# Attention and a depthwise convolution on one core: column differences of the last tile on GpSimd, rows moved by transfers, a later factor pass

## The chip, the cores and the metric

The kernel runs on one core of a Trainium2 chip. The metric is the device time of one execution in microseconds; lower is better. Several executions are timed and the median is given. One further execution is recorded by the hardware profiler; its page and trace are what is read here.

## The reference

The input `x` has 16 images of 384 channels, 32 by 32 points, in float32. Two layers follow each other.

```python
def _gn(v, G=32, eps=1e-5):          # 32 groups of 12 channels
    g = v.reshape(B_, G, C_ // G, H_, W_)
    m = jnp.mean(g, axis=(2, 3, 4), keepdims=True)
    s = jnp.var(g, axis=(2, 3, 4), keepdims=True)
    return ((g - m) / jnp.sqrt(s + eps)).reshape(v.shape)

x = x + attention(_gn(x))            # 8 heads of 48 channels over 1024 points
w_sym = (w + rot90(w) + rot90(w, 2) + rot90(w, 3)) * 0.25
x = x + depthwise_conv7x7(_gn(x), w_sym)   # one 7 x 7 filter per channel, padding 3
```

The filter is the mean of its four rotations. So it has the same value at (dy, dx) and (-dy, -dx), and each tap can be taken as a part that is even in dx and one that is odd in dx: sums and differences of columns.

## The kernel before

**Tiles.** A tile is 128 channels by 1024 points of one image; an image has three. Attention runs image by image on TensorE with the exponentials on ScalarE. The convolution of an image runs beside the attention of the next ones. VectorE convolves all tiles but three. The three of `PE_TILES` go to TensorE: tile 2 of image 14 (called the first below), then tiles 2 and 1 of image 15. Tile 0 of image 15 is `LAST`, the last tile of VectorE.

**VectorE's way to convolve a tile** (`fold_ops`). The tile lies in `padded`, rows of 32 points with a pitch of 35. `side(j, n, op)` (line 865) makes the sum or the difference of the columns at +j and -j, one `TENSOR_TENSOR` of 128x1024. `into` (line 868) adds a side times a weight to a row buffer, `rows_e` for the even part and `rows_o` for the odd one; `shifted` (lines 882 and 884) adds a row buffer, moved by dy rows, to the output tile. Line 884 is the plain addition; line 882 is taken once `scale` has been filled and multiplies by a factor at the same time.

**The last image is special.** Its normalization factors are known only late. So its tiles are convolved without them, and the factors are put in at the end. `whole` (line 889) is the factor pass of `LAST`: it multiplies the output tile by the factor and adds `rest`, a buffer that holds the tile itself plus a border term. What `shifted` adds after `whole` must carry the factor, by line 882. For `LAST`, ScalarE makes the first term of each odd row buffer (`begin`, line 962), with the sides that VectorE has made just before.

**The factors.** ScalarE sums each channel of image 15 (`moments`); TensorE averages over groups twice (`average`, line 400): first the means, and then, once VectorE has made `d` (lines 411 to 413), the variances. VectorE makes line 417, GpSimd the power (line 418), VectorE lines 421 and 1714. Then ScalarE writes the border terms (line 1727), and GpSimd's queue adds them to `rest` and to the two TensorE tiles (line 1728, accumulating transfers).

**TensorE's way to convolve a tile.** The image's rows are loaded several times at different offsets into the `sh` buffers (`conv_load`, lines 1092 and 1094, eight transfers each), and matmuls with banded matrices follow (`conv_on_pe`, line 1115). The result lies in PSUM with even and odd rows of a channel on different partitions. ScalarE copies it to SBUF (`conv_take`, line 1130), and `conv_perm` brings the rows to their channel by four matmuls with a permutation (line 1141). ScalarE copies that to an SBUF tile (line 1156 with the factor, line 1160 without it), GpSimd's queue adds it to the tile of `x` (line 1161), and SP's queue stores the sum (line 1175). The very last tile, (15, 1), is added by VectorE from PSUM instead (`conv_add`, line 1171), and ScalarE's queue stores it.

**What sets the order.** Every engine runs its instructions in the order in which the program issues them, and waits on semaphores for others. The program is written by a planner with two clocks, one for TensorE and one for VectorE: `after(wait, cost, f)` puts a small piece of work at a due time, `catch_up(to)` issues VectorE's next operations up to a time, with the costs that stand beside them in the list `ops`. The end of the program (`fast_end`) is written by hand: it issues the moments, the copy `rest` (line 1681), the pieces of TensorE's convolution and the two averages; `first` holds the permutations of the first tile until the factors are known. Transfers are issued by SP, ScalarE and GpSimd, each in its own order; a transfer that waits holds back all behind it on its queue.

Of the kernel before, what the change touches and what calls it, by code (L numbers as in the profile page):

```python
# [10 lines left out]
F32 = mybir.dt.float32  # L11
I32 = mybir.dt.int32
AF = mybir.ActivationFunctionType
# [32 lines left out]
def kernel(  # L46
# [96 lines left out]
    def run(general):  # L143
        tag = "g" if general else "f"
        with ExitStack() as stack:
# [710 lines left out]
            def fold_ops(b, k, i):  # L856
# [16 lines left out]
                scale = []  # L873

# [47 lines left out]
                slot = {2: 0, 3: 1, 1: 2}  # L922
                for n, (dy, (j, l)) in enumerate(((1, (2, 3)), (2, (3, 1)), (3, (1, 2)))):
                    sums.append(
                        (ts, lambda dy=dy, j=j, n=n: first(rows_o[n % 2], sides[slot[j]], o(dy, j)))
                    )
                    sums.append(
                        (full, lambda dy=dy, l=l, n=n: into(rows_o[n % 2], sides[slot[l]], o(dy, l)))
                    )
                    out_rows(lambda n=n: rows_o[n % 2], dy, ALU.subtract)  # L930
# [28 lines left out]
                if (b, k) == LAST:  # L959

                    def begin(n, dy, j):
                        nc.scalar.activation(rows_o[n], sides[slot[j]], AF.Identity, scale=o(dy, j))  # L962

                    def side_begin(j, n, dy):
                        side(j, n, ALU.subtract)
                        begin(n, dy, j)

                    def minus_begin():
                        shifted(rows_o[0], -1, ALU.subtract)
                        begin(0, 3, 1)  # L970

                    ops = [op for op in ops if op[1] not in [f for _, f in (*sums[12:], *outs[10:])]]
                    ops += [
                        (full, lambda: side_begin(2, 0, 1), None),
                        (full, lambda: side_begin(3, 1, 2), None),
                        (full, lambda: (sums[14][1](), other_borders()), None),
                        (*sums[16], None),
                        (*sums[18], None),
                        (*outs[10], None),
                        (full, minus_begin, None),  # L980
                        (full, whole, None),
                        (*outs[12], None),
                        (*outs[13], None),
                        (*sums[20], None),
                        *((*f, None) for f in outs[14:]),
                    ]
                return ops

# [143 lines left out]
            def conv_perm(b, k, a):  # L1132

                nonlocal clock
                if a == 0:
                    return
                pss[b, k] = psum(f"ps_rows_{b}_{k}")
                for half in range(2):
                    part = slice(64 * half, 64 * half + 64)
                    for row in range(2):  # L1140
# [8 lines left out]
                if (b, k) == PE_TILES[-1]:  # L1149
                    after(5.0, 1.5, lambda: conv_add(b, k))  # L1150
                    return
                t = tpool.tile([P, N], F32, tag="t", name=f"conv_{b}_{k}")
                if b == B - 1:
                    while "borders" not in late:
                        catch_up(now() + 0.5)
                    nc.scalar.activation(
                        by_rows(t), grids(pss[b, k]), AF.Identity, scale=ends["st"].sc[:, k, 0:1]
                    )
                else:
                    nc.scalar.copy(by_rows(t), grids(pss[b, k]))  # L1160
# [503 lines left out]
            def fast_end(b):  # L1664
# [16 lines left out]
                nc.scalar.copy(grid(ends["x"]), padded_view(n))  # L1681
                after(4.0, 0.3, check_end)
# [179 lines left out]
```

## Time and profile before

| | |
|---|---|
| median of 3 runs | 2838.41 us (2837.36 to 2839.85) |
| the profiled execution | 2837.61 us |
| its span, first to last instruction | 2835.8 us |
| TensorE busy | 2823.5 us (100% of the span) |
| VectorE busy | 2080.8 us (73%) |
| ScalarE busy | 1665.1 us (59%) |
| GpSimd busy | 271.5 us (10%) |
| granted TensorE clock | 0.999 |

In the profile PE is TensorE, DVE is VectorE, ACT is ScalarE, POOL is GpSimd and SP is the sync engine, which issues transfers. A row of a timeline gives the start and the duration in us from the start of the span, then engine, line, operation, the tile that is written and those that are read, their shapes, and the number of instructions that are merged in the row; in brackets stands the idle time before it and what ended it. The busy shares say nothing of the end of the program. There the stretches are:

| stretch, us | TensorE busy | VectorE busy | ScalarE busy | GpSimd busy | mean DMA share |
|---|---|---|---|---|---|
| 2783 to 2799 | 16.00 | 15.93 | 14.17 | 0.00 | 0.50 |
| 2799 to 2810 | 11.00 | 10.89 | 1.60 | 2.58 | 0.41 |
| 2810 to 2828 | 16.50 | 16.82 | 10.20 | 3.65 | 0.90 |
| 2828 to 2836 | 0.00 | 0.20 | 0.00 | 0.00 | 0.47 |

### The profile page before, as it was taken

Reading aid. Unit: us, or ns where it says so; the run is one execution under the profiler, and the core shown is the slowest. Engines: PE = TensorE matmul, PEld = TensorE weight load, DVE = VectorE, ACT = ScalarE, POOL = GpSimd, SP = SyncE. Lnnn points to the kernel's source line nnn. Section 1 sums busy time; section 2 is a strip of 40 time slices with the busy share of each in tenths; the row PEclk is TensorE's granted clock in tenths of the full one; section 3 lists DMA queues with packets and bytes.
Section 4 is the critical chain, followed back from the end, with each engine's and each line's share of the span. In section 5 each row is a group of like instructions: output and inputs, shape, how many; then the busy total and the mean of one; then the engine's idle time right before and its main releaser. Section 6 shows DMA issues by size and latency. Waiting matters only on the chain. (4 is left out here: it accounts for less than half of the span.)

```text
span 2835.8 us, 46155 instructions
## 1 busy us (share of the span) xinstructions
PE 2823.5 (100%) x19356; PEld 1122.2 (40%) x19356; DVE 2080.8 (73%) x2264; ACT 1665.1 (59%) x1954; POOL 271.5 (10%) x450
## 2 busy tenths in 40 slices
PE   9999999999999999999999999999999999999998
PEld 5344343433434334343443434334343343434433
DVE  5502968959598595976959689595985959869788
ACT  3637647376574756647466474765747566474653
POOL 4201011310100001010010100101000010100111
PEclk9999999999999999999999999999999999999999
DMA  6512031211212112121120302112121121211224
GB/s 238 188 37 50 27 81 26 54 50 45 64 32 44 50 44 64 34 64 43 37 65 27 82 24 51 50 44 65 32 44 50 44 64 33 63 45 37 72 72 136
DMA packets 75994, 168.21 MB, mean 59 GB/s; under 512 B 32416, under 2 KB 34400, under 8 KB 74240
## 3 DMA queue, kind: packets, MB, share of 16 engines
q0 software_dynamic: 33856, 111.00, 15.1%
q1 hardware_dynamic: 40912, 52.32, 6.8%
q8 instruction: 154, 2.52, 0.4%
q10 hardware_dynamic: 1008, 1.84, 0.2%
q14 instruction: 64, 0.52, 0.1%
HBM read 112.37 MB, written 27.43 MB: 49 GB/s over the span
## 5 line engine op out<-in xcount | busy, mean ns | idle before, releaser
L646 ACT ACTIVATE e<-ps_s 128x1024 f32<-128x1024 f32 x1024 | 1021.7, 1030 | 448.8 <-PE ps_s L638 443.2
L638 PE MATMUL ps_s<-qk 48*64 48x512 f32 x8192 | 1041.1, 589 | 0.0
L658 PE MATMUL acc<-e,v 64*64 64x512 f32 x8192 | 1040.1, 588 | 0.0
L865 DVE TENSOR_TENSOR side<-padded 128x1024 f32<-128x1024 f32 x270 | 328.6, 1218 | 338.2 <-ACT padded L836 338.2
L868 DVE SCALAR_TENSOR_TENSOR rows_e<-side,even,rows_e 128x1024 f32<-128x1024 f32 x405 | 509.3, 1273 | 85.6 <-ACT rows_e L847 84.0
L638 PEld LDWEIGHTS ps_s<-qk 48*64 48x64 f32 x8192 | 311.0, 132 | 574.3 <-issue 526.5
L658 PEld LDWEIGHTS acc<-e,v 64*64 64x64 f32 x8192 | 312.8, 132 | 569.6 <-issue 569.6
L567 PE MATMUL ps_qk<-x,wqk 128*128 128x512 f32 x1152 | 501.3, 594 | 1.4 <-DVE x L483 1.4
L567 PEld LDWEIGHTS ps_qk<-x,wqk 128*128 128x128 f32 x1152 | 217.6, 190 | 278.5 <-issue 271.3
L884 DVE TENSOR_TENSOR x<-x,rows_e 128x992 f32<-128x992 f32 (+2 forms) x270 | 310.6, 1150 | 0.0
L884 DVE TENSOR_TENSOR x<-x,rows_o 128x992 f32<-128x992 f32 (+2 forms) x266 | 305.1, 1147 | 3.0
L574 ACT COPY qk<-ps_qk 128x1024 f32<-128x1024 f32 x96 | 97.2, 1012 | 318.9 <-PE ps_qk L567 318.9
L593 PE MATMUL ps_v<-wv,x 128*128 128x384 f32 x768 | 252.6, 486 | 0.0
L719 PE MATMUL ps_proj<-o,wp 128*128 128x512 f32 x540 | 234.2, 592 | 0.0
L613 ACT COPY v<-ps_v 64x384 f32<-64x384 f32 x256 | 121.6, 475 | 122.4 <-PE ps_v L593 119.8
L593 PEld LDWEIGHTS ps_v<-wv,x 128*128 128x128 f32 x768 | 145.9, 190 | 108.2 <-issue 14.3
L868 DVE SCALAR_TENSOR_TENSOR rows_o<-side,odd,rows_o 128x1024 f32<-128x1024 f32 x135 | 172.7, 1280 | 2.0 <-ACT rows_o L962 0.5
L994 POOL DMA_DIRECT2D out<-x x44 | 24.9, 565 | 1545.1 <-DVE x L884 1544.4
L868 DVE SCALAR_TENSOR_TENSOR x<-side,even,x 128x1024 f32<-128x1024 f32 x135 | 172.4, 1277 | 0.0
L719 PEld LDWEIGHTS ps_proj<-o,wp 128*128 128x128 f32 x540 | 102.6, 190 | 126.2 <-issue 117.7
L727 ACT ACTIVATE x<-ps_proj,bp 128x1024 f32<-128x1024 f32 x45 | 50.1, 1114 | 167.5 <-PE ps_proj L719 167.5
L847 ACT ACTIVATE rows_e<-padded,even 128x1024 f32<-128x1024 f32 x135 | 146.8, 1167 | 0.0
(177 smaller groups left out, 1045.7 us busy)
## 6 DMA issues: line engine op xcount, KB each, us to landing
x<-in_x POOLq DMA_DIRECT2D x90, 512.0 KB, 5.4
inv<-inv SPq DMA_DIRECT2D x126, 256.0 KB
out<-x POOLq DMA_DIRECT2D x44, 512.0 KB, 3.0
xs<-in_x POOLq DMA_DIRECT2D x42, 512.0 KB, 6.4
qk<-qk POOLq DMA_DIRECT2D x96, 128.0 KB, 4.1
o<-o SPq DMA_DIRECT2D x180, 32.0 KB
sh<-v SPq DMA_DIRECT2D x32, 128.0 KB
sum<-o SPq DMA_DIRECT2D x128, 4.0 KB
```

The costliest lines, as they stand in the source:

```text
L567: nc.tensor.matmul(ps[:, h, :], lhsT=wqk[:, k, s, t, :], rhs=xns[b][:, k, h * HALF : (h + 1) * HALF], start=(k == 0), stop=(k == NK - 1),)
L574: nc.scalar.copy(halves(qks[u][:, s, :]), ps)
L593: nc.tensor.matmul(ps[:, j, 0:C], lhsT=xns[b][:, k, t * P : (t + 1) * P], rhs=wv[:, k, :], start=(k == 0), stop=(k == NK - 1),)
L613: nc.scalar.copy(dst[:, :, 0 : HEADS // 2 * (D + 1)].rearrange("p k (h d) -> p k h d", d=D + 1)[:, :, :, 0:D], src.rearrange("p k (h d) -> ...
L638: nc.tensor.matmul(ps[64 * c : 64 * c + 64, a, :], lhsT=qk[r, 1, 64 * kb : 64 * kb + 64], rhs=qk[r, 0, h * HALF : (h + 1) * HALF], start=True,
L646: nc.scalar.activation(es[n], ps, AF.Exp, scale=SCALE)
L658: nc.tensor.matmul(accs[a][64 * j : 64 * j + 64, :], lhsT=v[rows, kb, c : c + 64], rhs=e[rows, j, :], start=(kb == 0), stop=(kb == 2 * NT ...
L719: nc.tensor.matmul(ps[:, h, :], lhsT=wp[:, t, o * P : (o + 1) * P], rhs=os_[b, t // 2][:, t % 2, h * HALF : (h + 1) * HALF], start=(t == 0 ...
L847: nc.scalar.activation(grid(rows_e[dy - 1]), padded_view(i), AF.Identity, scale=even[:, k, dy, 0:1],)
L865: vec.tensor_tensor(grid(sides[n]), padded_view(i, j), padded_view(i, -j), op)
L868: vec.scalar_tensor_tensor(dst, src, w, dst, ALU.mult, ALU.add)
L884: vec.tensor_tensor(dst, dst, src, op)
```

## The change

It has three parts, all in the work on the last image.

First, the three column differences of `LAST` are made by GpSimd into buffers of their own (`ends["minus_sides"]`, in two buffers of the pool that held attention's outputs), issued in `fast_end` right after the copy `rest`. The two scaled copies that begin the odd row buffers follow at once on ScalarE (`odd_begin`, which takes the place of `begin`).

Second, the permutation matmuls of TensorE's first tile, (14, 2), are replaced by 16 transfers on SP's queue (`conv_rows_by_dma`), SBUF to SBUF, 16 partitions of 512 elements each, into `planes`. ScalarE's copy, GpSimd's accumulation and SP's store of that tile are issued after those of tile (15, 2). The loops of the remaining permutations are swapped: row outside, half inside.

Third, `whole` moves behind the two additions with dy = 2, which are therefore plain ones (line 884) and no longer carry the factor. So four additions of the odd part precede it.

```diff
+                slot = {2: 0, 3: 1, 1: 2}
+
+                def minus(j):
+                    return ends["minus_sides"][j] if (b, k) == LAST else sides[slot[j]]
...
-                    def side_begin(j, n, dy):
-                        side(j, n, ALU.subtract)
-                        begin(n, dy, j)
-
                     def minus_begin():
                         shifted(rows_o[0], -1, ALU.subtract)
-                        begin(0, 3, 1)
+                        odd_begin(0, 3, 1)
...
                     ops += [
-                        (full, lambda: side_begin(2, 0, 1), None),
-                        (full, lambda: side_begin(3, 1, 2), None),
-                        (full, lambda: (sums[14][1](), other_borders()), None),
-                        (*sums[16], None),
+                        (full, lambda: (sums[16][1](), other_borders()), None),
                         (*sums[18], None),
                         (*outs[10], None),
                         (full, minus_begin, None),
-                        (full, whole, None),
                         (*outs[12], None),
                         (*outs[13], None),
+                        (full, whole, None),
                         (*sums[20], None),
...
+            def odd_begin(n, dy, j):
+
+                nc.scalar.activation(
+                    rows_o[n],
+                    ends["minus_sides"][j],
+                    AF.Identity,
+                    scale=odd[:, LAST[1], dy, j : j + 1],
+                )
...
+                if (b, k) == PE_TILES[0]:
+                    conv_rows_by_dma(b, k)
+                    return
                 pss[b, k] = psum(f"ps_rows_{b}_{k}")
-                for half in range(2):
-                    part = slice(64 * half, 64 * half + 64)
-                    for row in range(2):
+                for row in range(2):
+                    for half in range(2):
+                        part = slice(64 * half, 64 * half + 64)
...
+                while "borders" not in late:
+                    catch_up(now() + 0.5)
+                conv_out(b, k, pss[b, k])
+                conv_out(*PE_TILES[0], ends["planes"])
+
+            def conv_rows_by_dma(b, k):
+
+                rows = epool.tile([P, 2, HALF], F32, tag="e", name=f"planes_{b}_{k}")
+                for half in range(2):
+                    for i in range(NG // 2):
+                        for row in range(2):
+                            first = 2 * CG * i + CG * (1 - row)
+                            nc.sync.dma_start(
+                                rows[64 * half + i : 64 * half + 64 : NG // 2, row, :],
+                                shs[b, k][first : first + CG, half, :],
+                            )
+                ends["planes"] = rows
+
+            def conv_out(b, k, rows):
...
                 ends["x"] = flat(epool.tile([P, 2, HALF], F32, tag="e", name="rest"))
                 nc.scalar.copy(grid(ends["x"]), padded_view(n))
+                free = [oqpool.tile([P, 2, N], F32, tag="oq", name=f"minus_{n}") for n in range(2)]
+                ends["minus_sides"] = minus = {}
+                for i, j in enumerate((2, 3, 1)):
+                    minus[j] = free[i // 2][:, i % 2, :]
+                    nc.gpsimd.tensor_tensor(
+                        grid(minus[j]), padded_view(n, j), padded_view(n, -j), ALU.subtract
+                    )
+                odd_begin(0, 1, 2)
+                odd_begin(1, 2, 3)
                 after(4.0, 0.3, check_end)
```

`conv_out` holds the lines that ended `conv_perm` before: ScalarE's copy, GpSimd's accumulation and SP's store of a tile.

More of the change, by code (lines that the diff above doesn't have):

```diff
@@ L921, in fold_ops @@
                     sums.append((full, lambda j=j, n=n: side(j, n, ALU.subtract)))
-                slot = {2: 0, 3: 1, 1: 2}
                 for n, (dy, (j, l)) in enumerate(((1, (2, 3)), (2, (3, 1)), (3, (1, 2)))):
                     sums.append(
-                        (ts, lambda dy=dy, j=j, n=n: first(rows_o[n % 2], sides[slot[j]], o(dy, j)))
+                        (ts, lambda dy=dy, j=j, n=n: first(rows_o[n % 2], minus(j), o(dy, j)))
                     )
                     sums.append(
-                        (full, lambda dy=dy, l=l, n=n: into(rows_o[n % 2], sides[slot[l]], o(dy, l)))
+                        (full, lambda dy=dy, l=l, n=n: into(rows_o[n % 2], minus(l), o(dy, l)))
                     )
@@ L959, in fold_ops @@
                 if (b, k) == LAST:
-                    def begin(n, dy, j):
-                        nc.scalar.activation(rows_o[n], sides[slot[j]], AF.Identity, scale=o(dy, j))
-                    def side_begin(j, n, dy):
-                        side(j, n, ALU.subtract)
-                        begin(n, dy, j)
                     def minus_begin():
                         shifted(rows_o[0], -1, ALU.subtract)
-                        begin(0, 3, 1)
+                        odd_begin(0, 3, 1)
                     ops = [op for op in ops if op[1] not in [f for _, f in (*sums[12:], *outs[10:])]]
                     ops += [
-                        (full, lambda: side_begin(2, 0, 1), None),
-                        (full, lambda: side_begin(3, 1, 2), None),
-                        (full, lambda: (sums[14][1](), other_borders()), None),
-                        (*sums[16], None),
+                        (full, lambda: (sums[16][1](), other_borders()), None),
                         (*sums[18], None),
@@ L1151, in conv_perm @@
                     return
+                while "borders" not in late:
[14 more added lines that the diff above has]
+            def conv_out(b, k, rows):
                 t = tpool.tile([P, N], F32, tag="t", name=f"conv_{b}_{k}")
                 if b == B - 1:
-                    while "borders" not in late:
-                        catch_up(now() + 0.5)
                     nc.scalar.activation(
-                        by_rows(t), grids(pss[b, k]), AF.Identity, scale=ends["st"].sc[:, k, 0:1]
+                        by_rows(t), grids(rows), AF.Identity, scale=ends["st"].sc[:, k, 0:1]
                     )
                 else:
-                    nc.scalar.copy(by_rows(t), grids(pss[b, k]))
+                    nc.scalar.copy(by_rows(t), grids(rows))
                 nc.gpsimd.dma_start(x1s[b, k], t, accum_op=ALU.add)
```

## Prediction

> **What bounds the kernel now.** I read the page first. TensorE is busy for 2823.5 of 2835.8 us at full clock, so over most of the span nothing can be won elsewhere. The change, however, touches only the last tile pieces of image 15 and one of image 14, all after 2783 us. So the question is which engine ends that stretch, and I read the timelines of the engines there. The view of the chain that ended last holds just the closing additions L1171; they are where VectorE and TensorE meet.
>
> TensorE (start, duration, engine, line, operation, count):
>
> ```profile
> 2799.25 1.72 PE L400 MATMUL ps_st_x<-mo_x,wv 128*128 128x1 f32 x14
> 2804.32 1.72 PE L400 MATMUL ps_st_x<-d_x,wv 128*128 128x1 f32 x14
> 2805.97 1.94 PE L1141 MATMUL ps_rows<-rows,perm 128*64 128x512 f32 x8
> ...
> 2823.80 2.71 PE L1141 MATMUL ps_rows<-rows,perm 128*64 128x512 f32 x8
> ```
>
> TensorE has no gap between these rows. 2805.97 is the permutation that the change removes; 2823.80 is the last one, which the closing additions read.
>
> VectorE in the same stretch:
>
> ```profile
> 2783.66 1.22 DVE L865 TENSOR_TENSOR side<-padded 128x1024 f32<-128x1024 f32 x1
> ...
> 2801.47 0.16 DVE L413 TENSOR_TENSOR d_x<-d_x,mo_x 128x3 f32<-128x3 f32 x1
> ...
> 2809.67 3.49 DVE L865 TENSOR_TENSOR side<-padded 128x1024 f32<-128x1024 f32 x3
> 2813.64 2.48 DVE L868 SCALAR_TENSOR_TENSOR rows_o<-side,odd,rows_o 128x1024 f32<-128x1024 f32 x2 [0.47 <-ACT rows_o L962]
> ...
> 2824.73 1.32 DVE L882 SCALAR_TENSOR_TENSOR x<-rows_o,mo_x,x 128x416 f32<-128x416 f32 x2
> 2826.54 1.66 DVE L1171 SCALAR_TENSOR_TENSOR x<-ps_rows,sc_x,x 128x256 f32<-128x256 f32 x4 [0.50 <-PE ps_rows L1141]
> ```
>
> VectorE runs without a pause from 2783.66, ends its own tile at 2826.05 and waits only 0.50 us for TensorE's permutation. So two engines end the kernel together: each must get shorter for the end to move. After L1171 (2828.2) come the last stores, the branch and the closing barriers, 7.6 us up to 2835.8, which I carry over.
>
> **The change, part by part.** *1. Three subtractions leave VectorE.* From 2809.67 to 2813.64, 3.97 us go (three L865 and the 0.47 us wait). *2. The factor pass L889 moves behind four additions:* the two 960-column updates become plain additions. Two L882 of that width take 2819.80 to 2822.20, 2.40 us; two L884 of 960 columns go by at about 1.07 us, 2.14 us. Saved 0.26 us. L889 also waits for the border term that GpSimd's queue adds to `rest`. Together VectorE saves 4.23 us, and without anything else would end its tile at 2821.8.
>
> *3. One permutation leaves TensorE:* 1.94 us by its row, on the path. The swapped loops (row outside, half inside) move no work; in the last permutation the second matmul now waits for ScalarE's copy where the third did. Between -0.4 and +0.3 us; I take 0. TensorE alone would end at 2826.5 - 1.9 = 2824.6, which beats VectorE's 2821.8, so without a collision the end moves by **-1.9 us**.
>
> *4. The rows go by 16 transfers on SP's queue*, 16 partitions by 512 elements each, behind the 32 `sh` loads and ahead of the stores. The trace has that shape, L708:
>
> ```profile
> 2599.38 3.71 SPq L708 DMA_DIRECT2D o<-o  x6
> ...
> 2783.27 23.52 SPq L1094 DMA_DIRECT2D sh<-v  x32
> ```
>
> 3.71 / 6 = 0.62 us each, 9.9 us, so SP issues them from 2806.8 to 2816.7; landed by about 2819 (estimate: 2 us more, as the small GpSimd transfers `gs_x<-ch_x` show). The one reader is ScalarE's copy of those planes, now in front of its two copies of the last TensorE tile. ScalarE gets there at 2817 without a collision and at 2823 with the one below, while TensorE needs the second of those copies only at 2822 or 2825. Cost 0; if the planes came after 2821, each us late would be a us on the path. Then this tile's accumulating transfer is the last on GpSimd's queue and its store the last on SP's, no longer early as before:
>
> ```profile
> x<-conv POOLq DMA_DIRECT2D x2, 512.0 KB, 4.9
> x<-border POOLq DMA_DIRECT2D x2, 512.0 KB, 6.7
> ```
>
> *5. Two scaled copies (L962) move up on ScalarE* behind the copy `rest` (ends 2796.98): 2.2 us, ending 2799.2, if GpSimd is done with its second subtraction. Queued behind are the row copies; the urgent one waits for TensorE until 2799.4 anyway. Free.
>
> *6. Three subtractions of 128x1024 on GpSimd*, starting once `padded` is whole (2782.9). No row has this operation at this size. Nearest from below: clearing 128x1126 takes 1.03 us, so 0.94 us for 1024. From above, the Trainium skill (GPSIMD Engine Reference, Performance versus the Vector engine) gives 4497 ns for a two-input addition of 2048 float32; half is an estimate of 2.25 us, plus a wait of one VectorE operation (1.2 us). I take 2.25 us: with two inputs to read and one to write it is nearer to that than to a clearing. Three end near 2790, well before ScalarE asks (2797) and before GpSimd's L418 (2806), so by this count alone they are free. The trace speaks against that:
>
> ```profile
> 14.36 2.00 POOL L1532 MEMSET padded<- 128x1126 f32 x2
> ...
> 14.63 2.28 DVE L483 TENSOR_SCALAR x<-x,sc_x 128x1024 f32<-128x1024 f32 x1
> ...
> 506.67 7.93 POOL L1050 TENSOR_TENSOR eye<-eye,ident 128x16 f32<-128x16 f32 x7
> ...
> 13.50 0.89 POOL L475 TENSOR_TENSOR sc_x<-d_x,mhalf 128x3 f32<-128x3 f32 x1 [3.32 <-DVE ge_x L476]
> ...
> 2806.32 1.87 POOL L418 TENSOR_TENSOR sc_x<-d_x,mhalf 128x3 f32<-128x3 f32 x1 [34.05 <-DVE d_x L417]
> ```
>
> The first of the two L483 lasted 2.28 us where the like L871 lasts 0.75: it stood until both clearings had ended at 16.36, then ran. The seven L1050 are 16 columns wide and still take 1.1 us each, the beat of VectorE's operations beside them; L418 took 1.87 us beside VectorE, L475 0.89 with VectorE idle. So the two engines shut each other out. The skill (SBUF — State Buffer, Who interferes with whom) has the rule: a VectorE operation with two SBUF inputs and a GpSimd operation that reads SBUF use one port pair, locked for a whole instruction; whichever comes second stands still. The rows show VectorE held by GpSimd only for an operation of another kind; the rule extends it to this one. By the first rows taken as cost alone the sum is -1.9 us; by the rule GpSimd starts at 2783.0 while VectorE is on an operation that reads PSUM, and VectorE's next, L865 at 2783.66, has two SBUF inputs. It stands until 2783.0 + 3 x 2.25 = 2789.75, or between single operations for the same total: **6.1 us**. I take the rule.
>
> **The sum.** All VectorE work shifts by 6.1 us: L413 ends at 2807.7 instead of 2801.6. TensorE's second group average (L400, 2804.32) needs it and stands 3.5 us, with all later matmuls behind it in order. TensorE's end: +3.5 - 1.9 = +1.6, at 2828.1. VectorE's tile: 2826.05 + 6.1 - 4.23 = 2827.9. L1171 then ends at 2829.8, **+1.6 us**. The scales come at about 2814.7, the border terms' transfers go at 2816.8 to 2819.6, and L889, due at 2822.8, finds `rest` landed (2816.8 + 6 = 2822.8). ScalarE has the rows scaled and copied by 2823.9. GpSimd's accumulations start when the border of the same tile has landed, 2818.1 + 6.7 = 2824.8, and one after the other; they land at 2829.7 and 2830.7, and SP's last store leaves at about 2830.8 against 2828.0 before. SP has read the branch value earlier by then, which gives back about 1 us of the 2.8. So the end moves between +1.6 and +2.8; I take **+2.1 us**. In the profiled execution: span 2835.8 + 2.1 = 2837.9, and with the 1.8 us around it 2839.7. That execution (2837.61) lies 0.8 below the median of the runs shown, so on the median's scale 2838.41 + 2.1 = **2840.5 us**, +0.07%.
>
> **The rivals.** What a measurement of this kernel can tell from no change is about 0.2%, 5.7 us.
> A, the above, chance 0.60: 2838.5 to 2843.
> B, no collision: GpSimd's reads slip in beside VectorE. For it: the 128x16 operations of GpSimd slowed VectorE's neighbours by only some 0.02 us each. Against: they are tiny, and L483 stood. Then TensorE alone ends the kernel, -1.9 us: 2836.5. Chance 0.20.
> C, slower by over 0.2%: a GpSimd subtraction costs much more than 2.25 us and holds the port all the while. Each us above 2.25 is paid three times on VectorE, and TensorE stands along: +2.1 + 3(T - 2.25) passes 5.7 from T = 3.45 us. At 4.5 us, twice my value, it is +8.9: 2847.3. For it: inputs with a row pitch of 35, no such row in the trace. Against: the estimate comes from a stated duration. Chance 0.15.
> D, the late tile: the 16 transfers or the two accumulations meet in the busy DMA stretch (mean busy share 0.90 from 2810 to 2828), and SP's last store leaves 3 us later than in A: 2843.5. Chance 0.05.
>
> **How the numbers follow.** The predicted time is A's. Faster by over 0.2% needs under 2832.7: nothing above reaches it, 0.02. Slower, over 2844.1: C and a little of D, 0.16. Same 0.82. The range takes in A, B and D and the nearest edge of C: 2835.5 to 2845.5, leaving out about 0.15.
>
> **What would show it.** Right: the first L865 after `padded` starts near 2789 or is stretched, VectorE work to that point is about 6 us late, and TensorE has a gap before the second group average. GpSimd's three rows end before 2792. Wrong (B): L413 still ends near 2801.6 and L1171 waits for TensorE by more than 2 us. C: GpSimd rows over 3.4 us. D: ScalarE waits for the planes, or SP's last store leaves after 2833.

## The result and the profile after

The changed kernel takes **2843.09 us** (median of 22 runs, 2841.30 to 2846.01); the kernel before takes 2838.18 us on the same chip (22 runs). The ratio is 1.0017, with a 95% interval of 1.0011 to 1.0023: 4.9 us slower, within 0.2% but not equal. The prediction was 2840.5 us (2835.5 to 2845.5), so the sign and the range held and the size fell short by 2.6 us.

The profiled execution took 2843.09 us, with a span of 2841.4 us against 2835.8. Of these 5.6 us, 1.4 have nothing to do with the change: `padded` is whole 1.41 us later, a difference that arises in the first 250 us, where both programs are identical. It differs from one profiled execution to the next (from 1.2 us earlier to 5.6 us later than before among the kernels below). So in all that follows times stand **from the start of the last L781 that writes `padded`** (2782.13 us before, 2783.54 us after). On this clock the kernel before ends at 53.67 and the changed one at 57.86: **4.2 us** to explain.

The timeline of TensorE after (start, duration, engine, line, operation, shapes, count, and in brackets the idle time with what ended it); L1117 is L1115 of before, L1146 is L1141:

```profile
2800.66 1.72 PE L400 MATMUL ps_st_x<-mo_x,wv 128*128 128x1 f32 x14
2802.31 3.48 PE L1117 MATMUL ps_conv<-sh,mat 128*32 128x512 f32 x32
2807.59 1.72 PE L400 MATMUL ps_st_x<-d_x,wv 128*128 128x1 f32 x14 [1.79 <-DVE d_x L413]
2809.24 4.29 PE L1117 MATMUL ps_conv<-sh,mat 128*32 128x496 f32 x24
...
2826.85 2.70 PE L1146 MATMUL ps_rows<-rows,perm 128*64 128x512 f32 x8
```

The permutation behind the second average is gone, and a gap of 1.79 us stands before that average. The last permutation starts at 43.31 on the common clock, 41.67 before: +1.64 us. That is the predicted +1.6, but not for the predicted reason. The 24 matmuls behind the average took 4.29 us; before, the same 24 took 2.63:

```profile
2807.84 2.63 PE L1115 MATMUL ps_conv<-sh,mat 128*32 128x496 f32 x24
```

The view of stretches shows why (TensorE, weight loads, VectorE, ScalarE and GpSimd busy, granted clock, DMA share, GB/s):

```profile
2805.80:2807.60 1.80, 0.01 (x1) 0.02 (x1) 1.73 (x6) 0.00 (x0) 0.00 (x0) 1.00 0.61 211
2807.60:2809.20 1.60, 1.60 (x14) 1.60 (x14) 1.60 (x2) 0.00 (x0) 0.00 (x0) 1.00 0.32 79
2809.20:2812.70 3.50, 3.50 (x21) 1.01 (x25) 3.50 (x5) 0.00 (x0) 0.49 (x1) 0.51 0.18 42
2812.70:2818.00 5.30, 5.30 (x59) 1.56 (x52) 5.27 (x8) 3.99 (x9) 2.45 (x3) 1.00 0.25 57
2818.00:2825.00 7.00, 7.00 (x64) 1.93 (x56) 6.86 (x7) 4.57 (x6) 2.08 (x3) 1.00 1.06 201
...
2832.00:2837.00 5.00, 0.00 (x0) 0.00 (x0) 0.00 (x0) 0.00 (x0) 0.00 (x0) 0.61 1.01 374
```

The granted clock fell to 0.51 for 3.5 us after the gap. So TensorE paid 1.8 us for the wait and 1.7 us for the clock, and won 1.9 us.

The timeline of VectorE after:

```profile
2785.07 2.35 DVE L865 TENSOR_TENSOR side<-padded 128x1024 f32<-128x1024 f32 x1
2787.34 2.44 DVE L871 TENSOR_SCALAR x<-padded,even 128x1024 f32<-128x1024 f32 x1
2789.70 2.91 DVE L865 TENSOR_TENSOR side<-padded 128x1024 f32<-128x1024 f32 x1
...
2807.37 0.16 DVE L413 TENSOR_TENSOR d_x<-d_x,mo_x 128x3 f32<-128x3 f32 x1
...
2829.59 1.66 DVE L1193 SCALAR_TENSOR_TENSOR x<-ps_rows,sc_x,x 128x256 f32<-128x256 f32 x4 [1.75 <-PE ps_rows L1146]
```

The first L865 has its usual start but takes 2.35 us, against 1.22; the L871 behind it 2.44 against 0.75; the next L865 2.91 against 1.22. Together 4.5 us. L413 starts at 23.83, 4.5 us later than before. The closing additions (L1193, before L1171) end at 47.71, before at 46.07: +1.64 us.

The timelines of GpSimd and of SP in the kernel after; POOL's and SP's transfers stand there with the time that the engine spends on issuing them:

```profile
2784.43 7.10 POOL L1708 TENSOR_TENSOR minus<-padded 128x1024 f32<-128x1024 f32 x3 [10.75 <-issue]
...
2816.44 0.93 POOL L1759 DMA_DIRECT2D rest<-border  x1 [2.35 <-ACT border L1758]
2817.87 0.87 POOL L1759 DMA_DIRECT2D x<-border  x1 [0.50 <-ACT border L1758]
2819.30 0.85 POOL L1759 DMA_DIRECT2D x<-border  x1 [0.56 <-ACT border L1758]
2824.51 1.73 POOL L1183 DMA_DIRECT2D x<-conv  x2 [4.36 <-ACT rows L1132]
```

```profile
2784.67 21.86 SPq L1096 DMA_DIRECT2D sh<-v  x32
2806.65 10.85 SPq L1169 DMA_DIRECT2D planes<-rows  x16
2830.41 3.27 SPq L1197 DMA_DIRECT2D out<-x  x2
```

In the kernel before, GpSimd's transfers and SP's two stores, of which the second left at 2828.0, were:

```profile
2809.29 0.93 POOL L1161 DMA_DIRECT2D x<-conv  x1 [1.09 <-ACT conv L1160]
...
2816.37 0.85 POOL L1728 DMA_DIRECT2D x<-border  x1 [2.63 <-ACT border L1727]
...
2823.08 0.85 POOL L1161 DMA_DIRECT2D x<-conv  x1 [4.42 <-DVE x L882]
```

```profile
2813.87 14.50 SPq L1175 DMA_DIRECT2D out<-x  x2
```

The three subtractions end at 2791.5, VectorE's operations between them included. Two accumulations of convolutions (`x<-conv`) now go one behind the other, and two stores behind them. The second store leaves at 49.8 on the common clock; before, SP's last store left at 45.9. These 3.9 us, and not the 1.64 of the closing additions, make up most of the 4.2. The DMA view says how long the transfers took to land (KB each, median us); before they took 6.7 and 4.9:

```profile
x<-border POOLq DMA_DIRECT2D x2, 512.0 KB, 8.7
x<-conv POOLq DMA_DIRECT2D x2, 512.0 KB, 7.1
```

Of the two `x<-conv` the first took 5.8 us and the second 8.3. So they landed at 46.8 and 49.8; the single one of before landed at 45.9.

### The profile page after: what moved, and what is told of

Read it like the earlier page. It is cut to its first block, busy times and chain, and to the rows that moved or that the text cites. A ratio compares the mean times of both kernels' runs of the same rounds, so it can differ in the third digit from the quotient of the medians.

```text
span 2841.4 us, 46164 instructions
## 1 busy us (share of the span) xinstructions
PE 2824.1 (99%) x19348; PEld 1123.6 (40%) x19348; DVE 2081.8 (73%) x2261; ACT 1663.9 (59%) x1954; POOL 284.1 (10%) x453
## 3 DMA queue, kind: packets, MB, share of 16 engines
q0 software_dynamic: 33856, 111.00, 15.1%
## 5 line engine op out<-in xcount | busy, mean ns | idle before, releaser
L865 DVE TENSOR_TENSOR side<-padded 128x1024 f32<-128x1024 f32 x267 | 329.2, 1233 | 338.8 <-ACT padded L836 338.8
```

Source lines behind the costliest of these rows:

```text
L865: vec.tensor_tensor(grid(sides[n]), padded_view(i, j), padded_view(i, -j), op)
```

## The experiments

Twelve kernels were run, each beside the kernel before on the same chip. The table gives the ratio to the kernel before, and from each trace, on the common clock: when the border term of tile (15, 2) is sent, when the convolutions of (15, 2) and of (14, 2) are sent to be added, and the end.

| kernel | ratio (95%) | border of (15, 2) | conv of (15, 2) | conv of (14, 2) | end |
|---|---|---|---|---|---|
| before | | 34.24 | 40.95 | 27.16 | 53.67 |
| after | 1.0017 (1.0011 to 1.0023) | 34.33 | 40.97 | 41.5 | 57.86 |
| e1, differences alone | 1.0015 (1.0009 to 1.0022) | 35.68 | 43.30 | 30.68 | 56.59 |
| e3, no differences | 1.0006 (0.9998 to 1.0015) | 32.82 | 38.64 | 41.71 | 55.46 |
| e4, clears | 1.0010 (1.0002 to 1.0018) | 30.30 | 37.56 | 42.71 | 56.40 |
| e5, first tile first | 1.0017 (1.0010 to 1.0025) | 34.35 | 41.02 | 39.33 | 58.14 |
| e6, average later | 1.0019 (1.0010 to 1.0027) | 35.42 | 42.74 | 43.3 | 59.92 |
| e7, no late accumulation | 1.0013 (1.0007 to 1.0020) | 35.45 | 41.97 | none | 58.50 |
| e8, rows early | 1.0030 (1.0019 to 1.0040) | 44.06 | 49.79 | 37.27 | 63.49 |
| e9, differences twice | 1.0040 (1.0026 to 1.0054) | 40.81 | 47.30 | 47.8 | 63.79 |
| e10, border early | 1.0004 (0.9995 to 1.0012) | 32.16 | 41.37 | 27.16 | 54.57 |
| e11, border first | 1.0001 (0.9993 to 1.0009) | 30.73 | 37.46 | 27.16 | 53.91 |
| e12, one border less | 1.0002 (0.9993 to 1.0010) | 34.25 | 40.99 | 27.15 | 54.45 |
| e13, one border less, after | 1.0019 (1.0010 to 1.0027) | 34.33 | 41.29 | 41.8 | 59.18 |

None of them is faster than the kernel before. In every trace but e7's, SP's last store leaves within 0.1 us of the landing of the last accumulation, and the end comes 7.3 to 9.7 us behind that store. This last piece differs so much from trace to trace that a difference of the ends under about 1 us says little.

### The collision: GpSimd clears instead of subtracting (e4)

```diff
-                    nc.gpsimd.tensor_tensor(
-                        grid(minus[j]), padded_view(n, j), padded_view(n, -j), ALU.subtract
-                    )
+                    nc.gpsimd.memset(minus[j], 0.0)
```

GpSimd still writes the buffers, but reads nothing. So it doesn't wait for `padded`, and two of the three clears run earlier. The odd part of `LAST` is left out of the output by this.

> The changed kernel with GpSimd's three subtractions replaced by clears of the same tiles, which write and read nothing; the odd part of the last VectorE tile is thus left out of the result (zero differences), while every instruction of the other engines stays. Theory (the lock is on reading, as the skill has it): the additions with two inputs beside the clears keep 1.2 us and only the tensor_scalar waits, by about 1.2 us; TensorE has no gap; about as E3, 2837.5 to 2839.5. Rival (any work on GpSimd holds VectorE): the first addition is stretched by about 2 us too.

The timeline of VectorE in e4, at the same place:

```profile
2785.33 1.22 DVE L865 TENSOR_TENSOR side<-padded 128x1024 f32<-128x1024 f32 x1
2786.46 0.75 DVE L871 TENSOR_SCALAR x<-padded,even 128x1024 f32<-128x1024 f32 x1
2787.12 1.22 DVE L865 TENSOR_TENSOR side<-padded 128x1024 f32<-128x1024 f32 x1
```

And that of GpSimd:

```profile
2779.58 1.84 POOL L1708 MEMSET minus<- 128x1024 f32 x2 [5.64 <-issue]
2784.68 0.95 POOL L1708 MEMSET minus<- 128x1024 f32 x1 [3.26 <-PE ps_proj_last L767]
```

Without the subtractions the three operations take 1.22, 0.75 and 1.22 us, as before the change: the subtractions made the stretching. Rival B of the prediction, no collision, is out. What e4 can't show is that it comes from GpSimd's reads. The Trainium skill has it so (SBUF — State Buffer, Who interferes with whom: a VectorE operation with two SBUF inputs contends with a GpSimd operation that reads SBUF, and not with one that only writes it). But two clears had ended 3.9 us before the first L865 began, and the third ran beside it for only 0.3 us. That it wasn't stretched agrees with the skill, on thin ground. The expected wait of the L871 was not put to the test, since GpSimd was idle by then.

Without the collision the border terms left 4.0 us earlier than after. The time was above what was expected, 2842.32 us, and the end came only 1.5 us earlier than after, because another wait took over, in the timeline of ScalarE in e4:

```profile
2825.18 1.04 ACT L1182 COPY conv<-planes 128x1024 f32<-128x1024 f32 x1 [6.13 <-DMA planes<-rows]
```

ScalarE stood 6.13 us for the rows that SP moves. Their 16 transfers took 14.06 us to issue (0.88 each), with the border terms' accumulations among them; they took 10.85 us (0.68 each) after, where these accumulations come later. So the row transfers are hidden in the changed kernel only because the collision makes everything else later.

### The collision doubled (e9)

```diff
+                    for _ in range(2):
                         nc.gpsimd.tensor_tensor(
                             grid(minus[j]), padded_view(n, j), padded_view(n, -j), ALU.subtract
                         )
```

> The changed kernel with each of GpSimd's subtractions made twice. Theory (the two engines lock each other out for whole instructions): VectorE loses about 9 to 10 us at its first operations instead of 4.5, the second group average waits some 6.5 to 7 us instead of 1.8, everything behind it shifts by about 5 us, and the time is 4.5 to 6 us above the changed kernel. Rival (the two engines only share the port, with a limit on what VectorE loses): less than 2 us above it.

The timeline of GpSimd in e9:

```profile
2787.01 15.68 POOL L1709 TENSOR_TENSOR minus<-padded 128x1024 f32<-128x1024 f32 x6 [10.75 <-issue]
```

Six subtractions take 15.68 us, with VectorE's operations between them. `d` is ready 9.3 us later than before (28.66 against 19.34), against 4.5 us with three subtractions, TensorE stands 6.61 us before the second average, and the end comes 5.9 us later than after. So the three added ones cost VectorE 4.8 us, the first three 4.5: about **1.5 us of VectorE's time for each subtraction**. The forecast loss of VectorE and wait of TensorE hold; the time is 6.9 us above the changed kernel's by the medians, where 4.5 to 6 were expected. So the chain from the subtractions over VectorE and the second average to the border terms (6.5 us later than after) and the end is shown.

### Each part alone (e1, e3)

e1 is the changed kernel with the permutation and the place of the factor pass as before; e3 is the kernel before with the row transfers and the later factor pass. Against after and before:

```diff
 # e1
-                if (b, k) == PE_TILES[0]:
-                    conv_rows_by_dma(b, k)
-                    return
...
                         (full, minus_begin, None),
+                        (full, whole, None),
                         (*outs[12], None),
                         (*outs[13], None),
-                        (full, whole, None),
 # e3
+                if (b, k) == PE_TILES[0]:
+                    conv_rows_by_dma(b, k)
+                    return
...
-                        (full, whole, None),
                         (*outs[12], None),
                         (*outs[13], None),
+                        (full, whole, None),
```

> Part 1 alone: GpSimd makes the three differences; permutation, stores and factor pass as before. Theory (GpSimd and VectorE shut each other out): the three VectorE operations beside GpSimd stretch by 4.5 us in all as in the changed kernel, the second group average waits about 1.8 us and TensorE's clock then drops to half for 3.4 us, so TensorE ends 3.5 us later than before and the kernel is 3 to 4.5 us slower, 2841.2 to 2842.7. Rival (the late rows and their store cost all of the loss): within 1 us of before.

> Parts 2 and 3 without part 1: VectorE makes its differences again. Theory: no VectorE operation is stretched, TensorE has no gap and ends 1.9 us earlier than before; VectorE ends 0.3 us earlier; the closing additions end about 0.7 us earlier than before, but SP's last store leaves 2 to 3 us later than before, so the time is 0 to 2 us above before, 2838.2 to 2840.2. Rival (the late rows cost all of the loss): 4 to 5 us above before.

e1 is 3.6 us slower than before by the medians (2842.8 against 2839.2), without any row transfer. Its TensorE had the same gap of 1.79 us, but behind it stood the permutation, which took 3.61 us at a granted clock of 0.51 instead of 1.94, and the closing additions ended 5.5 us later than before (51.61), where 3.5 were expected. VectorE even waited 2.06 us for `rest` in front of the factor pass.

e3 is 2.1 us slower (2841.33 against 2839.2), although it takes 1.94 us from TensorE and adds nothing to VectorE. Its interval takes in no change, and the time lies just above what was expected; but the closing additions, which were to end 0.7 us earlier than before, end 2.5 us later (48.55). The timeline of ScalarE in e3 has the reason:

```profile
2824.61 1.04 ACT L1180 COPY conv<-planes 128x1024 f32<-128x1024 f32 x1 [5.12 <-DMA planes<-rows]
```

The planes come late by 5.12 us. Behind this copy stand the last scaled copy, for which VectorE waits, and the accumulation of (14, 2), which was sent at 27.16 before and goes at 41.71. In the changed kernel ScalarE doesn't wait for the planes: the collision covers this lateness. The two parts' losses are 2.9 and 1.8 us in the traces, 4.7 in sum; that both together cost 4.2 is a difference within the scatter.

### The gap and the clock (e6)

```diff
-                    pe_conv.extend(((b, k, 0, 0, KS), (b, k, 1, 0, 4), (b, k, 1, 4, KS)))
+                    pe_conv.extend(((b, k, 0, 0, KS), (b, k, 1, 0, 6), (b, k, 1, 6, KS)))
```

Six groups of taps instead of four go ahead of the second average, so that TensorE has work while VectorE is late.

> The changed kernel with two more groups of matmuls (1.7 us) of tile (15, 2) ahead of the second group average, so that TensorE has work while it waits for VectorE. Theory (the end is set by the last accumulating transfer and SP's store behind it, not by TensorE): TensorE's gap and its half clock disappear, the closing additions end 1.2 to 1.9 us earlier than in the changed kernel, but SP's last store leaves as before, and the time falls by less than 1 us: 2842.3 to 2843.3 on a chip where before has 2838.2. Rival (TensorE's late end is what costs): the time falls by 1.5 to 3 us.

The timeline of TensorE in e6:

```profile
2803.55 5.12 PE L1117 MATMUL ps_conv<-sh,mat 128*32 128x512 f32 x48
2808.82 1.72 PE L400 MATMUL ps_st_x<-d_x,wv 128*128 128x1 f32 x14 [0.15 <-DVE d_x L413]
2810.48 0.99 PE L1117 MATMUL ps_conv<-sh,mat 128*32 128x464 f32 x8
```

The wait is 0.15 us, and the eight matmuls behind the average take 0.99 us, 0.12 each, where the 24 took 0.18 each in the changed kernel. The closing additions end 1.24 us earlier than after (46.47). Yet the end comes **2.1 us later**, and the time is no better than after's (ratio 1.0019 against 1.0017): neither the theory's gain nor the rival's. The average starts where it did after (24.0 on the common clock), but the scales and the border terms come 1.1 us later, because VectorE reads the average later. Its L417 went at 2811.98 after (28.4) and goes here at 29.6:

```profile
2814.41 0.15 DVE L417 TENSOR_SCALAR d_x<-ps_st_x 128x3 f32<-128x3 f32 x1
```

The planner has put one more of VectorE's operations in front of it. This was the first sign that the closing additions don't set the end of the changed kernel: the border terms' path does.

### The order of the last transfers (e5, e10, e11)

e5 is the changed kernel with the first tile's accumulation and store ahead of those of (15, 2). e10 is the kernel before with the border of (15, 2) sent right behind that of `rest`. e11 is the kernel before with the later factor pass, and that border ahead of that of `rest`.

```diff
 # e5
+                conv_out(*PE_TILES[0], ends["planes"])
                 conv_out(b, k, pss[b, k])
-                conv_out(*PE_TILES[0], ends["planes"])
 # e10
                 add_border(0, ends["x"])
+                add_border(PE_K[0], x1s[B - 1, PE_K[0]])
...
-                    for k in PE_K:
+                    for k in PE_K[1:]:
 # e11
-                add_border(0, ends["x"])
+                add_border(PE_K[0], x1s[B - 1, PE_K[0]])
...
+                    add_border(0, ends["x"])
-                    for k in PE_K:
+                    for k in PE_K[1:]:
```

> The changed kernel with the copy, accumulation and store of tile (14, 2) issued ahead of those of (15, 2). Theory (the late store of (14, 2) adds some 2 us behind the closing additions): SP's last store leaves about 1.5 to 2 us earlier against the closing additions, and the time falls by 1 to 2.5 us against the changed kernel, 2840.6 to 2842.1. Rival (the end is set by the closing additions alone): no change, 2843.

> The kernel before, with the border term of (15, 2) made right behind that of rest, ahead of the two scaled copies L962. Theory (the end of the kernel before is set by SP's store of (15, 2), which waits for two accumulating transfers in turn; the closing additions have over 2 us to spare): the accumulation of (15, 2) starts near 39 us after padded is whole instead of 40.95, SP's store leaves near 43.7 instead of 45.9, VectorE's additions end about 1 to 1.5 us later, and the time falls by 1 to 2 us. Rival (the closing additions set the end): 1 to 1.5 us slower.

> The kernel before with part 3 of the change (factor pass behind four additions), and the border term of (15, 2) made ahead of that of rest. Theory: the accumulation of (15, 2) starts near 37.5 us after padded is whole, SP's store leaves near 42.5; rest lands later, so the factor pass waits 1 to 2 us and the closing additions end up to 1.5 us later; the time falls by 1 to 2.5 us. Rival (the closing additions set the end): 0.5 to 1.5 us slower.

None of the three moves the end to the good. In e5 the accumulation of (14, 2) leaves 2.2 us earlier than after, that of (15, 2) at the same time, and the end is 0.3 us later; the time is that of after, as its rival had it. In e10 the border of (15, 2) leaves 2.1 us earlier than before, but its tile's convolution is sent 0.4 us later: it followed the border by 9.2 us instead of 6.7, because the border took 8.7 us to land, beside the transfer for `rest` and a store that had left 1.4 and 0.4 us ahead of it. In e11 the convolution is sent 3.5 us earlier, but takes 7.9 us to land among the other transfers, and SP's last store leaves only 0.5 us earlier. An earlier start of one transfer in a stretch where the DMA share is near 1 is paid by the others.

The time of e10 (1.0 us above before) is what its rival forecast, and in both kernels the closing additions end later than before, by 0.9 and 1.0 us. So these two don't decide which path ends the kernel before, where SP's last store (45.9) and the closing additions (46.07) lie close together. e1 speaks for the store: there the end came only 4.98 us behind the closing additions, against 7.6 before.

### One accumulation less (e7, e12, e13)

By then I held that the number of accumulating transfers of 512 KB between the scales and SP's last store sets the end: four took about 15.1 us from the first to SP's last store, in before, e1 and e8 (though 16.1 in e10 and 14.6 in e11), and five 16.6 us or more. Three kernels take one out. e7 is the changed kernel without the accumulation of (14, 2); that tile then lacks its convolution. e12 and e13 are the kernels before and after without the accumulation of the border term of (15, 1).

```diff
 # e7
-                nc.gpsimd.dma_start(x1s[b, k], t, accum_op=ALU.add)
+                if (b, k) != PE_TILES[0]:
+                    nc.gpsimd.dma_start(x1s[b, k], t, accum_op=ALU.add)
 # e12, e13
-                nc.gpsimd.dma_start(dst, t, accum_op=ALU.add)
+                if k != PE_K[1]:
+                    nc.gpsimd.dma_start(dst, t, accum_op=ALU.add)
```

> The changed kernel with the accumulating transfer of tile (14, 2) left out: that tile is stored without its convolution; all other work stays. Theory (two accumulating transfers of 512 KB at the busy end set it): the accumulation of (15, 2) lands in about 5 us instead of 5.9, SP's last store leaves near 46 us after padded is whole instead of 49.8, and the kernel is 2 to 3 us faster than the changed kernel, about 2 us above before. Rival (the closing additions set the end): within 0.5 us of the changed kernel.

> The kernel before, with the accumulating transfer of the border term of tile (15, 1) left out: that tile then lacks its border term. ScalarE still makes the term. Three accumulations instead of four lie between the scales and SP's last store. Theory (the accumulating transfers of the last stretch set the end): SP's last store leaves 1.1 to 1.7 us earlier than the 45.9 us after `padded` of the kernel before, the closing additions stay where they are (46.1, they wait for TensorE), and the time falls by 1 to 1.7 us. Rival (the closing additions on VectorE set the end): the time stays within 0.3 us.

> The changed kernel, with the same accumulating transfer (border term of tile (15, 1)) left out: that tile lacks its border term. Four accumulations instead of five lie between the scales and SP's last store. Theory (accumulations set the end): SP's last store leaves about 15.1 us after the first of them, near 48.0 us after `padded` instead of 49.8, while the closing additions stay at 47.7; the time falls by 1.5 to 2 us against the changed kernel and is 3 us above the kernel before. Rival (closing additions set the end): no change against the changed kernel, 4.9 us above the kernel before.

**The count is wrong.** e12 takes the same time as before (2837.49 against 2837.41), e13 is no faster than after (1.0019 against 1.0017), and SP's last store hardly moves (46.2 against 45.9, and 49.5 against 49.8). These are the times of the rival, too; that the closing additions don't set the end of the changed kernel rests on e6 and e1. In e12's view of stretches (last column GB/s) one sees what the removed transfer leaves behind:

```profile
2818.00:2819.00 1.00, 1.00 (x16) 0.39 (x12) 0.96 (x2) 1.00 (x3) 0.00 (x0) 1.00 1.03 193
2819.00:2820.00 1.00, 1.00 (x16) 0.26 (x8) 0.96 (x2) 0.64 (x1) 0.00 (x0) 1.00 0.73 135
2820.00:2821.00 1.00, 1.00 (x16) 0.34 (x12) 1.00 (x1) 0.00 (x0) 0.00 (x0) 1.00 0.06 12
2821.00:2822.00 1.00, 1.00 (x16) 0.31 (x12) 1.00 (x2) 0.00 (x0) 0.06 (x1) 1.00 0.00 0
2822.00:2823.00 1.00, 1.00 (x9) 0.19 (x2) 0.96 (x2) 0.25 (x1) 0.81 (x1) 1.00 0.00 0
2823.00:2824.00 1.00, 1.00 (x6) 0.54 (x5) 0.96 (x2) 0.34 (x1) 0.00 (x0) 1.00 0.69 131
```

The DMA engines stand idle for three microseconds before GpSimd's next transfer has its data under way. GpSimd sends the convolution of (15, 2) at 2821.94, 6.74 us behind that tile's border term; in the kernel before it is 6.71 us, with or without the other transfer. The timeline of GpSimd in e13 names the wait:

```profile
2817.15 0.87 POOL L1760 DMA_DIRECT2D x<-border  x1 [0.49 <-ACT border L1758]
2824.11 1.75 POOL L1183 DMA_DIRECT2D x<-conv  x2 [6.09 <-DMA x<-border]
```

So what sets this place is a **chain on one tile**: the border term of (15, 2) is added to it, then the convolution is added to the same tile and must wait until the border has landed, then the tile is stored. The idle stretch is the end of the wait: in e12 the border's data stop at about 2820, the next transfer is sent at 2821.94, and its data begin after 2823. The border of (15, 1) fills this hole, and costs nothing there. (The Trainium skill, DMA: Bandwidth & Descriptors, Anatomy of one DMA, has about 2 us for setup and completion of a transfer apart from its data. The idle stretch holds one completion and the next setup, and is about 3 us. At the page's 436 GB/s, 512 KB would take 1.2 us, an estimate; here the stretch of accumulations from 2818 to 2825 after moved 201 GB/s, which is 2.6 us each.)

e7 is not clear. Its border terms left 1.1 us later than after, because the half clock fell on the second average too (2.73 us against 1.72), and the copy on ScalarE that stands ahead of them had to wait longer for TensorE; its closing additions ended 1.6 us later (49.34), and a dip to 121 GB/s opened where the accumulation had been. Counted from the border of (15, 2), SP's last store leaves 2.6 us earlier than after (12.9 against 15.5), but the end comes only 0.5 us earlier (23.05 against 23.53; before 19.43). By the medians it is 3.9 us above before, the changed kernel 4.9, with intervals that overlap; 2 to 3 us less than the changed kernel were expected. So the accumulation alone, without its tile's store, gave back at most about 1 us.

### The rows moved early (e8)

The kernel before with parts two and three, and the 16 transfers sent early, by GpSimd's and ScalarE's queues.

```diff
                 for p in perms:
                     conv_take(*p)
+                conv_rows_by_dma(*PE_TILES[0])
                 loads(1)
...
-                            nc.sync.dma_start(
+                            (nc.gpsimd, nc.scalar)[row].dma_start(
                                 rows[64 * half + i : 64 * half + 64 : NG // 2, row, :],
```

> Parts 2 and 3 without the differences on GpSimd, and the 16 row transfers issued right after ScalarE's copies by GpSimd's and ScalarE's queues, eight each, instead of behind the sh loads on SP's; the copy, accumulation and store of (14, 2) keep the early place that they have in before. Theory (the rows lose only by being late): no wait for the planes on ScalarE, no late store; TensorE ends 1.9 us earlier, VectorE 0.3 us; closing additions end 0.5 to 1 us earlier than before and SP's last store leaves as in before: time between -1 and +0.5 us of before. Rival (the transfers cost by themselves): 1.5 to 3 us above before, as E3.

A miss: 9.2 us slower than before. The view of SP's waits in e8 (what was waited for: us in all, times, longest):

```profile
SPq L1094 <- DMA planes<-rows: 11.4, 1, 11.4
```

SP's loads into `sh` waited 11.4 us for the row transfers to have read what the loads overwrite, and TensorE stood 8.28 us for these loads. The wait was moved, not removed. What the early transfers would bring without it was not tried.

## Why the prediction was right or wrong

**Sign and range right, the size 2.6 us short, and the sign in part by luck.** The collision that the prediction put at the centre is there, and TensorE waits for it. But the end of the changed kernel is late for another reason: the second accumulation at the end takes 2.9 us longer than forecast. Point by point:

1. *Subtractions off VectorE, and the factor pass (-4.23 us).* Right: VectorE had lost 4.5 us at L413, and its own tile ends 0.4 us later than before (44.30 against 43.92), so 4.1 us came back.
2. *The collision (6.1 us).* The mechanism was right, and shown by e4 and e9. The size was 4.5 us: the term T = 2.25 us per subtraction is the one that was mis-sized. In the prediction's own sum, three T less the 0.66 us by which GpSimd starts ahead of the first L865, 4.5 us stand for T = 1.7; six subtractions in e9, 9.3 us, give the same. GpSimd's first subtraction took 1.9 us. Rival C needed T above 3.45 us and is out, but the end does go along with VectorE: in e9, twice the subtractions cost 4.8 us more on VectorE and 5.9 us more at the end.
3. *TensorE, +3.5 - 1.9 = +1.6.* The sum was right (+1.64), its terms were not: the wait was 1.79 us, and the 1.7 us that were missing came from the clock at half speed, of which the prediction says nothing. Two errors cancelled, which is luck.
4. *The row transfers hidden.* Right in the changed kernel, at 0.68 us each instead of 0.62, ScalarE didn't wait for them. e3 and e4 show that the cover is thin: with everything else on time they cost 5 to 6 us of ScalarE's time.
5. *Scaled copies earlier on ScalarE, free.* Better than free. The scales came 4.5 us later than before (30.86 against 26.38), but the border of (15, 2) left at 34.33 against 34.24. Before, ScalarE came to the first border term 2.5 us behind the scales, since it waited for a piece of the convolution first, and two scaled copies (2.18 us) stood between the first term and the second. After, it is 0.2 us, and the three follow each other. This made up for the collision at this place.
6. *The end.* Here the prediction failed. The step "two engines end the kernel together", with the 7.6 us behind the closing additions carried over, doesn't hold: from the closing additions to the end it is 7.6 us before, 10.15 us after and 4.98 us in e1. Nor does VectorE run "without a pause": the prediction's own row has one of 0.47 us. The step that knew of the other path, "they land at 2829.7 and 2830.7, and SP's last store leaves at about 2830.8", is the one that was mis-sized: the second accumulation landed 3.0 us behind the first, not 1.0, and the first took 5.8 us, not 4.9. By the common clock the accumulations went 1.7 us *earlier* than forecast (40.97 is 2823.1 there, not 2824.8) and the second landed 8.8 us behind the sending of the first, not 5.9, so the last store left at 2831.9, 1.1 us later than forecast.

How the 4.2 us come about: up to the sending of the convolution of (15, 2) the two kernels are level (40.95 and 40.97). This accumulation lands 1.0 us later than before, in company (46.8 against 45.9); the one of (14, 2) lands 3.0 us behind it, and SP's last store waits for it; the rest to the end is 0.3 us longer. At some 200 GB/s the data of one accumulation are 2.6 us, an estimate that leaves little for anything else in the 3.0. Before, the accumulation of (14, 2) went at 27.16, when the DMA share was 0.01, and its store at 31.7. Now both come at the very end, where the DMA share is 1.

The other traces agree. Where (14, 2) is early, the end follows the sending of the convolution of (15, 2) by 12.7 to 13.8 us (before, e1, e8, e10, e12). Where it is late, it is 16.5 to 18.8 us (after, e3 to e6, e9, e13, and e7, where its store alone is left). e11 has it early and still takes 16.5; its convolution was sent early, among the border terms. Two things stay open. How the 4 us divide between the accumulation and the store of (14, 2) is not settled by e7. And no run takes the late tile alone away: e1 has it early, but it has the permutation back in the place where the clock is halved, sends its border terms 1.4 us later than before, and is 3.6 us above before all the same.

"SP has read the branch value earlier, which gives back about 1 us" failed too: from SP's last store to the end it is 7.77 us before and 8.06 us after.

Of the rivals, A had the stall, and D (2843.5 us) what was missing: the two accumulations meeting in the busy stretch. The measured 2843.09 us lie just beyond A's range and 0.4 from D's. D gave SP's last store 3 us beyond A; it was 1.1 us beyond A's on the common clock, and the 1 us that A counted as given back was missing. D had a chance of 0.05: the prediction asked of the transfers when they would be landed and never how long their data occupy the DMA engines.

The profile's 5.6 us, the common clock's 4.2 and the medians' 4.9 differ within the scatter of single executions and their offsets.

## What to carry to other kernels

When a transfer is moved from an idle stretch to the end, give it the time of its data at the rate which that kind of transfer reaches in the trace (here 200 GB/s for accumulations, 374 for the stores at the end), and look for the chain on one tile, add, wait until landed, add, store, before counting transfers. Work given to GpSimd may be paid by VectorE, here 1.5 us for a subtraction of 1.9, and a short stall of TensorE may be paid twice, here 1.8 us by the wait and 1.7 by the clock behind it. When an experiment takes a cause away, look in its trace where the replaced instructions ran: two of e4's three clears ran elsewhere. A step hidden by another step's lateness isn't free: take the cover away, as e4 does, to see its price.

## What was not expected of the hardware

- **A gap of 1.79 us halved TensorE's clock.** The granted clock was 0.51 for 3.5 us behind it, in the changed kernel as in e1, and 24 matmuls took 4.29 us instead of 2.63. In e5, e7 and e13 the same gap did the same (4.30, 4.91 and 4.19 us). With the gap filled (0.15 us, e6) the granted clock stayed at 1.00. The Trainium skill (TensorE: Matmul & The Clock Gate, What's actually happening) has the length, a free-running window of about 3.4 us, but speaks of a whole idle window ahead of the drop; here a gap of half a window, followed by 1.7 us of one-column matmuls, was enough. Whether these thin matmuls had a part in it was not tried; in e7 the drop began among them.
- **GpSimd and VectorE take turns.** Three subtractions in a row didn't hold VectorE for their whole length; the subtractions took 1.9, 2.9 and 2.3 us, and the three operations of VectorE between them were stretched by 1.1, 1.7 and 1.7 us. L871, with one SBUF input, was stretched as well, as the prediction had read off the like L483.
- **A removed transfer may free nothing.** In e12 and e13 two to three idle microseconds of all DMA engines took the place of 512 KB, and the end didn't move.
